# A depthwise convolution's last 128 channels: nine scaled copies on ScalarE summed on GpSimd, in place of block-diagonal matmuls on TensorE

## The chip, the core and the metric

The kernel runs on one core of a Trainium2 chip. The metric is the device time of one execution in microseconds. Before the change three runs gave 7132.22, 7134.73 and 7137.01 us: the median is 7134.73.

The engines are written as in the profile: PE is TensorE (PEld its weight loads), DVE is VectorE, ACT is ScalarE, POOL is GpSimd, SP is SyncE, which here only issues DMAs.

## The reference

The input x is fp32, 16 images of 56 x 56 pixels with 384 channels. Two residual layers follow each other, each behind a group normalisation over 32 groups of 12 channels (mean and variance over a whole image, no learned scale).

```
x = x + proj(dilated_attention(gn(x)))       # layer 0
x = x + conv3x3_depthwise(gn(x), sign(w))    # layer 1
```

- Layer 0: q, k and v are products with a 1152 x 384 matrix. The 384 channels form three sets of 128 with dilation 1, 2 and 3; each set has four heads of 32 channels. Each pixel attends to its nine neighbours at that dilation (zero padding): nine scores, a softmax over them, and the weighted sum of the nine v. Then a 384 x 384 projection and a bias.
- Layer 1: each channel is convolved with its own 3 x 3 kernel, whose nine weights are the signs of w clipped to -1 to 1. So a tap multiplies by 1, -1 or 0. Padding is one pixel of zeros around the normalised image.

## The kernel before

**Tiling.** An image is cut into 7 chunks of 8 rows (PX = 448 pixels), 112 chunks in all. Channels lie on the 128 partitions, in three groups j = 0, 1, 2 of 128 channels; pixels lie along the free dimension.

**Stages.** The loop at the end of the kernel (L487 to L499) calls seven stages for different chunks in one step n: stage_a for n+9 (load, transpose on PE, statistics of layer 0, write to DRAM scratch xd), stage_kv for n+2 (normalise on ACT, k and v products pkv on PE, ACT copies them into the padded tiles kv), stage_s for n+1 (q products pq; DVE products t of q and shifted k; PE sums t over each head with sel into one bank ps), stage_p for n-1 (projection po, residual and bias on DVE into xb, statistics of layer 1, write to the scratch x1d), stage_m for n+1 (softmax), stage_w for n (weighted sum of v), and stage_c for n-9 (the convolution). Layer 1 of an image can only begin when all of layer 0 of that image is done, since its normalisation needs the image's statistics: hence the distance of 9 chunks.

**stage_m.** ACT copies the scores from ps to sT (L349), PE transposes them (pt_s, L358), DVE subtracts the maximum, ACT takes the exponential (L366), DVE divides by the sum. The weights e are split into three bf16 terms: ACT casts (L374, L376), GpSimd subtracts (rest, L375, and the last term of e, L377). PE transposes the terms (pa, L382), ACT copies them (aT, L388).

**stage_w.** For each of the three sets and each of the nine taps, 27 times a chunk: PE spreads the tap's weight over its head's 32 channels (pb_a, L402, two PSUM banks), DVE multiplies by the shifted v (w, L405, five buffers), and GpSimd adds to the set's sum (y, L409: the first add of a set takes two taps, so 8 adds a set and 24 a chunk).

**stage_c.** One DMA brings the chunk's x1 (L446, one buffer). For each j three DMAs (L461) bring the rows shifted by -1, 0 and +1 for 32 channels at a time, so that tile z has 96 partitions, which are 3 row shifts x 32 channels, and four quarters q of 448 pixels; z_p has three buffers. ACT normalises each quarter (L463, mrz holds mean and scale in that layout); GpSimd clears the rows outside the image in the first and the last chunk of an image, before and after (L456, L467). PE then takes 12 matmuls per j (pc, L474): for each column shift kx and quarter q a 96 x 32 matrix kdiag, which has the three row taps on three stacked diagonals, so one matmul sums three taps. The profile counts each fp32 matmul as two records: 72 a chunk. DVE adds pc to x1 (L478). When all three j are there, PE transposes x1 back (pt_o, L482), ACT copies (osb, L484) and a DMA writes the output.

**What orders the work.** The framework's scheduler fixes, when the kernel is built, the order of instructions on each engine's queue, by its own estimate of when they become ready; it also puts in the waits. On the chip each queue runs in that order, and an instruction that waits holds those behind it. DMAs are all issued from SP's queue. Buffers of a pool come round in turn.

Of the kernel before, what the change touches and what calls it, by code (L numbers as in the profile page):

```python
# [8 lines left out]
F32 = mybir.dt.float32  # L9
BF16 = mybir.dt.bfloat16  # L10
AF = mybir.ActivationFunctionType
ALU = mybir.AluOpType
# [4 lines left out]
P = 128  # L17
HEADS = 4
HD = 32
NG = 3  # L20
NTAP = 9
NQ = 4
ROWS = 8
# [9 lines left out]
def dilated_attention_then_binary_conv(  # L33
# [20 lines left out]

    nc = tc.nc
    B, H, W, C = x.shape
    PX = ROWS * W
    NCH = H // ROWS  # L60
# [2 lines left out]
    SCALE = float(HD) ** -0.5  # L63
    DIL = (1, 2, 3)
    K3 = 3 * HD

    xf = x.rearrange("b h w c -> b (h w) c")
    of = out.rearrange("b h w c -> b (h w) c")

    const = ctx.enter_context(tc.tile_pool(name="const", bufs=1))  # L70
# [48 lines left out]
    bias = const.tile([P, NG], F32, name="bias")  # L119

    spread = const.tile([NR, NTAP, P], BF16, name="spread")

    kdiag = const.tile([K3, 3, NG * NQ, HD], F32, name="kdiag")
    with tc.tile_pool(name="setup", bufs=1) as setup:
        wq_in = setup.tile([P, 9, C], F32, name="wq_in")
        nc.sync.dma_start(wq_in, w_qkv.rearrange("(t p) c -> p t c", p=P))
        wp_in = setup.tile([P, 3, C], F32, name="wp_in")
        nc.scalar.dma_start(wp_in, w_proj.rearrange("(t p) c -> p t c", p=P))
        b_in = setup.tile([NG, P], F32, name="b_in")
        nc.scalar.dma_start(b_in, b_proj.rearrange("(j p) -> j p", p=P))  # L130
        k_in = setup.tile([K3, 3, NG * NQ], F32, name="k_in")
        for ky in range(3):
            for kx in range(3):
                nc.scalar.dma_start(
                    k_in[ky * HD : (ky + 1) * HD, kx, :],
                    w_conv[ky, kx].rearrange("(s c) m -> c (s m)", c=HD),
                )

        for cc in range(NG):
            for t3 in range(3):  # L140
                pt = ps_tr.tile([P, 512], F32, tag="tr", name="pt_wq")
                for i in range(3):
# [24 lines left out]

        kc = setup.tile([K3, 3, NG * NQ], F32, name="kc")
        nc.vector.tensor_scalar(kc, k_in, -1.0, 1.0, op0=ALU.max, op1=ALU.min)
        kp = setup.tile([K3, 3, NG * NQ], F32, name="kp")  # L170
        nc.vector.tensor_single_scalar(kp, kc, 0.0, op=ALU.is_gt)
        kn = setup.tile([K3, 3, NG * NQ], F32, name="kn")
        nc.vector.tensor_single_scalar(kn, kc, 0.0, op=ALU.is_lt)
        nc.vector.tensor_sub(kp, kp, kn)
        nc.vector.tensor_sub(kp, kp, kc)
        nc.vector.tensor_add(kp, kc, kp)
        eye3 = setup.tile([K3, HD], F32, name="eye3")
        nc.gpsimd.memset(eye3, 0.0)
        for ky in range(3):
            nc.gpsimd.affine_select(  # L180
                out=eye3, in_=eye3, compare_op=ALU.not_equal, fill=1.0, base=-ky * HD,
                pattern=[[-1, HD]], channel_multiplier=1,
            )
        for kx in range(3):
            nc.vector.tensor_tensor(
                kdiag[:, kx],
                kp[:, kx].unsqueeze(2).to_broadcast([K3, NG * NQ, HD]),
                eye3.unsqueeze(1).to_broadcast([K3, NG * NQ, HD]),
                ALU.mult,
            )  # L190

# [8 lines left out]
    y_p = ctx.enter_context(tc.tile_pool(name="y_p", bufs=5))  # L200
    s_p = ctx.enter_context(tc.tile_pool(name="s_p", bufs=1))
    a_p = ctx.enter_context(tc.tile_pool(name="a_p", bufs=4))
    z_p = ctx.enter_context(tc.tile_pool(name="z_p", bufs=3))
    x1_p = ctx.enter_context(tc.tile_pool(name="x1_p", bufs=1))
    o_p = ctx.enter_context(tc.tile_pool(name="o_p", bufs=2))
    st_p = ctx.enter_context(tc.tile_pool(name="st_p", bufs=2))

# [2 lines left out]
    for g, d in enumerate(DIL):  # L210
        kv.append([])
        for s in range(KV_SLOTS):
            t = const.tile([P, 2, ROWS + 2 * d, W + 2 * d], F32, name=f"kv_{g}_{s}")
            nc.gpsimd.memset(t[:, :, :, 0:d], 0.0)
            nc.gpsimd.memset(t[:, :, :, W + d : W + 2 * d], 0.0)
            kv[g].append(t)

    def rows(ap):
        return ap.rearrange("p (r w) -> p r w", w=W)

    stats0, stats1 = {}, {}
    xd, x1d = {}, {}
    mr0, mr1 = {}, {}
# [38 lines left out]
    def spread_stats(pair):  # L262
        pp = ps_tr.tile([P, 512], F32, tag="tr", name="pp")
        for j in range(NG):
            nc.tensor.matmul(pp[:, 2 * j : 2 * j + 2], gselT[:, j], pair[:, 0:2], start=True, stop=True)
        mr = st_p.tile([P, NG, 2], F32, tag="mr", name="mr", bufs=4)
        nc.vector.tensor_copy(mr.rearrange("p j s -> p (j s)"), pp[:, : 2 * NG])
        return mr
# [144 lines left out]
    def stage_p(n):  # L413

        b, c = divmod(n, NCH)
        if c == 0:
            stats1[b] = st_p.tile([P, NG, NCH, 6], F32, tag="stats1", name="stats1")
            x1d[b] = dr_p.tile([C, H * W], F32, tag="x1d", name="x1d")
        xb, y = xbs.pop(n), ys.pop(n)
        for j in range(NG):  # L420
            po = ps_mm.tile([P, 512], F32, tag="mm", name="po")
            for g in range(NG):
                nc.tensor.matmul(  # L423
                    po[:, :PX], wprojT[:, g, j * P : (j + 1) * P], y[g], start=(g == 0), stop=(g == NG - 1)
                )
            nc.vector.scalar_tensor_tensor(  # L426
                xb[:, j, :], po[:, :PX], bias[:, j : j + 1], xb[:, j, :], op0=ALU.add, op1=ALU.add
            )
            nc.vector.bn_stats(stats1[b][:, j, c, :], xb[:, j, :])
        nc.sync.dma_start(x1d[b].rearrange("(j p) n -> p j n", p=P)[:, :, c * PX : (c + 1) * PX], xb)  # L430
        if c == NCH - 1:
            pair = group_stats(stats1.pop(b))

            mr = spread_stats(pair)
            mrz = st_p.tile([K3, NG, NQ, 2], F32, tag="mrz", name="mrz")
            for ky in range(3):
                for q in range(NQ):
                    nc.sync.dma_start(mrz[ky * HD : (ky + 1) * HD, :, q, :], mr[q * HD : (q + 1) * HD, :, :])
            mr1[b] = mrz

    def stage_c(n):

        b, c = divmod(n, NCH)
        p0 = c * PX
        x1 = x1_p.tile([P, NG, PX], F32, tag="x1", name="x1")
        nc.sync.dma_start(x1, x1d[b].rearrange("(j p) n -> p j n", p=P)[:, :, p0 : p0 + PX])  # L446
        by_set = x1d[b].rearrange("(j q c) n -> j c q n", q=NQ, c=HD)
        for j in range(NG):
            z = z_p.tile([K3, NQ, PX], F32, tag="z", name="z")
            edges = []  # L450
            if c == 0:
# [5 lines left out]
            for ky in range(3):  # L457
                lo = W if c == 0 and ky == 0 else 0
                hi = PX - W if c == NCH - 1 and ky == 2 else PX
                q0 = p0 + (ky - 1) * W  # L460
                nc.sync.dma_start(z[ky * HD : (ky + 1) * HD, :, lo:hi], by_set[j][:, :, q0 + lo : q0 + hi])  # L461
            for q in range(NQ):
                nc.scalar.activation(  # L463
                    z[:, q], z[:, q], AF.Identity, bias=mr1[b][:, j, q, 0:1], scale=mr1[b][:, j, q, 1:2]
                )
            for edge in edges:
                nc.gpsimd.memset(edge, 0.0)  # L467
# [2 lines left out]
            for kx in (1, 0, 2):  # L470
                lo, hi = max(0, 1 - kx), W - max(0, kx - 1)
# [56 lines left out]
```

## Time and profile before

| | |
|---|---|
| median of three runs | 7134.73 us |
| the profiled execution | 7133.72 us, its span 7132.0 us |
| PE busy | 6613.3 us (93%) |
| DVE busy | 4458.9 us (63%) |
| POOL busy | 3364.4 us (47%) |
| ACT busy | 2324.5 us (33%) |
| convolution matmuls (L474) | 8064 records, 1093.8 us busy |
| normalisation for them (L463) | 1344 activations, 753 ns each |
| adds of the weighted sums (L409) | 2688, 1145 and 1136 ns each |
| convolution loads (z from x1d) | 912 DMAs of 224.0 KB, 4.4 us to landing |
| granted PE clock, mean | 0.954 |

The table is of one profiled execution; its span is 1.7 us shorter than its time, and the time is 1 us under the median of the runs. A group of the profile names the line, the engine and operation, output and inputs by the program's names, shapes and count; behind the first bar stand the busy time and the mean duration of one in ns, behind the second the time that the engine sat idle just before them, and what ended most of it. The busy time of matmuls counts overlapping ones once: the four quarters of a pc group run side by side, so 8064 records of 576 ns make only 1093.8 us. The chain is the work that ended last, followed back from the end, at each step to what released it.

### The profile page before, as it was taken

The numbers are of one execution on the slowest core, as the hardware profiler recorded it, in microseconds if no ns is written. First come the engines' busy times: TensorE is split into PE (matmuls) and PEld (weight loads), VectorE is DVE, ScalarE is ACT, GpSimd is POOL, SyncE is SP. The second block draws the span as 40 slices with busy tenths as digits, with TensorE's granted clock in tenths as the row PEclk, the third lists the DMA queues.
The fourth block names the chain that finished last, engine by engine and source line by source line (L and its number), as shares of the span: only waits on it lengthen the run. The fifth ranks groups of instructions, "written<-read, shape, count | busy, mean of one in ns | idle before, by whom it ended". The sixth has DMA issues, their size and how long they took to land.

```text
span 7132.0 us, 88786 instructions
## 1 busy us (share of the span) xinstructions
PE 6613.3 (93%) x30933; PEld 2670.5 (37%) x30933; DVE 4458.9 (63%) x6431; ACT 2324.5 (33%) x4025; POOL 3364.4 (47%) x3279
## 2 busy tenths in 40 slices
PE   6888999999999999999999999999999999999977
PEld 3333333333333333333333333333333333333322
DVE  3666666666666666666666666666666666666650
ACT  2112333333333333333333333333333333333324
POOL 1555444445554544444444555545444444445540
PEclk8889999999999999999999999999999999999977
DMA  3212344333443443344443444343334343333335
GB/s 119 75 55 67 109 117 116 114 108 112 117 114 109 116 113 107 110 113 116 113 114 108 113 113 117 114 115 110 108 110 115 111 116 113 109 98 94 94 96 136
DMA packets 617462, 770.82 MB, mean 108 GB/s; under 512 B 164915, under 2 KB 617014, under 8 KB 617014
## 3 DMA queue, kind: packets, MB, share of 16 engines
q1 hardware_dynamic: 613008, 764.54, 37.8%
q8 instruction: 245, 4.01, 0.2%
q14 instruction: 203, 1.66, 0.1%
q10 hardware_dynamic: 4006, 0.61, 0.1%
HBM read 462.04 MB, written 231.21 MB: 97 GB/s over the span
## 4 chain that ended last, share of the span: by engine, by line
PE 68%; POOL 18%; issue 7%; DVE 5%; DMA 2%; ACT 1%; SPq 0%; POOLq 0%; ACTq 0%; DVEq 0%
PE pkv L310 16%; POOL y L409 15%; PE ps L343 13%; PE po L423 12%; PE pq L330 12%; PE pc L474 6%; PE pb_a L402 4%; DVE w L405 3%; PE pa L382 2%; POOL e L377 1%; PE pt_o L482 1%; PE pt_s L358 1%; PE pt_x L282 1%; DMA z<-x1d 1%; DMA xin<-in_x_dram 1%
## 5 line engine op out<-in xcount | busy, mean ns | idle before, releaser
L409 POOL TENSOR_TENSOR y<-y,w 128x448 f32<-128x448 f32 x2352 | 2693.6, 1145 | 227.4 <-DVE w L405 71.8
L405 DVE TENSOR_TENSOR w<-pb_a,kv 128x448 f32<-128x448 f32 x3024 | 1800.2, 616 | 824.4 <-PE pb_a L402 620.7
L339 DVE TENSOR_TENSOR t<-pq,kv 128x1344 f32<-128x1344 f32 x1008 | 1557.9, 1555 | 951.0 <-PE pq L330 722.0
L310 PE MATMUL pkv<-xn,wqkvT 128*128 128x448 f32 x4032 | 1767.1, 556 | 0.0
L409 POOL TENSOR_TENSOR y<-w 128x448 f32<-128x448 f32 x336 | 381.7, 1136 | 2749.2 <-DVE w L405 2748.7
L474 PE MATMUL pc<-z,kdiag 96*32 96x440 f32 (+1 forms) x8064 | 1093.8, 576 | 38.6 <-ACT z L463 20.0
L402 PE MATMUL pb_a<-aT,spread 108*128 108x448 bf16 x3024 | 1002.4, 371 | 126.3 <-DVE w L405 121.7
L463 ACT ACTIVATE z<-z,mrz 96x448 f32<-96x448 f32 x1344 | 936.0, 753 | 425.0 <-DMA z<-x1d 422.1
L343 PE MATMUL ps<-t,sel 128*32 128x448 f32 x6048 | 963.5, 551 | 0.0
L423 PE MATMUL po<-y,wprojT 128*128 128x448 f32 x2016 | 941.6, 576 | 10.0 <-POOL y L409 10.0
L310 PEld LDWEIGHTS pkv<-xn,wqkvT 128*128 128x128 f32 x4032 | 743.0, 196 | 478.1 <-issue 448.2
L330 PE MATMUL pq<-xn,wqkvT 128*128 128x448 f32 x2016 | 870.4, 557 | 0.0
L313 ACT COPY kv<-pkv 128x448 f32<-128x448 f32 x672 | 360.1, 536 | 910.0 <-PE pkv L310 900.6
L402 PEld LDWEIGHTS <-spread 108*128 108x128 bf16 x3024 | 283.1, 101 | 894.1 <-issue 869.7
L423 PEld LDWEIGHTS po<-y,wprojT 128*128 128x128 f32 x2016 | 329.7, 189 | 623.4 <-issue 608.2
L330 PEld LDWEIGHTS pq<-xn,wqkvT 128*128 128x128 f32 x2016 | 353.5, 189 | 482.6 <-issue 472.5
L349 ACT COPY sT<-ps 128x448 f32<-128x448 f32 x112 | 59.6, 532 | 1434.8 <-PE ps L343 1434.8
L426 DVE SCALAR_TENSOR_TENSOR xb<-po,bias,xb 128x448 f32<-128x448 f32 x336 | 227.0, 676 | 303.4 <-PE po L423 303.3
L343 PEld LDWEIGHTS ps<-t,sel 128*32 128x32 f32 x6048 | 152.3, 108 | 657.4 <-issue 299.6
L474 PEld LDWEIGHTS pc<-z,kdiag 96*32 96x32 f32 x8064 | 224.2, 112 | 459.1 <-issue 354.1
L382 PE MATMUL pa<-ident_h,e 112*108 112x112 bf16 x1344 | 141.6, 259 | 246.9 <-POOL e L377 246.8
L478 DVE TENSOR_TENSOR x<-pc,x 128x448 f32<-128x448 f32 x336 | 207.3, 617 | 228.8 <-PE pc L474 221.2
(90 smaller groups left out, 3556.9 us busy)
## 6 DMA issues: line engine op xcount, KB each, us to landing
z<-x1d SPq DMA_DIRECT2D x912, 224.0 KB, 4.4
xin<-in_x_dram SPq DMA_DIRECT2D x112, 672.0 KB, 6.1
xd<-xa SPq DMA_DIRECT2D x112, 672.0 KB, 5.9
xb<-xd SPq DMA_DIRECT2D x112, 672.0 KB, 4.6
x1d<-xb SPq DMA_DIRECT2D x112, 672.0 KB, 3.1
x<-x1d SPq DMA_DIRECT2D x112, 672.0 KB, 5.4
out_dram<-osb SPq DMA_DIRECT2D x448, 168.0 KB, 2.1
kv<-kv SPq DMA_DIRECT2D x192, 186.0 KB, 2.3
```

What stands on the lines that cost most here:

```text
L310: nc.tensor.matmul(pq[:, :PX], wqkvT[:, cc, o0 : o0 + P], xn[:, cc, :], start=(cc == 0), stop=(cc == NG - 1))
L313: nc.scalar.copy(cur[:, which - 1, d : d + ROWS, d : d + W], rows(pq[:, :PX]))
L330: nc.tensor.matmul(pq[:, :PX], wqkvT[:, cc, g * P : (g + 1) * P], xn[:, cc, :], start=(cc == 0), stop=(cc == NG - 1))
L339: nc.vector.tensor_tensor(t.rearrange("p k (r w) -> p k r w", w=W), q3, k3, ALU.mult)
L343: nc.tensor.matmul(ps[32 * j : 32 * j + 32, :PX], sel[:, s0 : s0 + 32], t[:, kx, :], start=(i == 0), stop=(p + 4 >= NG * NTAP),)
L382: nc.tensor.transpose(pa[:NR, s * SUB : (s + 1) * SUB], e3[:, s * NG + g].rearrange("p t m -> p (t m)"), ident_h[:SUB, :SUB],)
L402: nc.tensor.matmul(pb[:, :PX], spread[:, o, :], aT, start=True, stop=True)
L405: nc.vector.tensor_tensor(rows(w), rows(pb[:, :PX]), vw, ALU.mult)
L409: nc.gpsimd.tensor_tensor(y, first if o == 1 else y, w, ALU.add)
L423: nc.tensor.matmul(po[:, :PX], wprojT[:, g, j * P : (j + 1) * P], y[g], start=(g == 0), stop=(g == NG - 1))
L463: nc.scalar.activation(z[:, q], z[:, q], AF.Identity, bias=mr1[b][:, j, q, 0:1], scale=mr1[b][:, j, q, 1:2])
L474: nc.tensor.matmul(pcr[q * HD : (q + 1) * HD, :, lo:hi], kdiag[:, kx, j * NQ + q, :], zr[:, :, lo + kx - 1 : hi + kx - 1], start=(kx == 1) ...
```

## The change

The convolution of j = 0 and 1 (JG = 2) stays as it was. For j = 2 there is another way:

- At set-up the signs of the nine taps of the last 128 channels are computed into ktap (128 channels x 9). kdiag shrinks to the first two groups. Two padded tiles zg (128 x 10 x 58) are allocated and cleared.
- In stage_c the load of x1 covers j = 0 and 1; a second DMA brings xg, the ten rows of the last 128 channels that the chunk needs (one buffer). ACT normalises xg into the inside of the padded tile zp with one activation. Then ACT makes nine scaled copies of shifted windows of zp, three for each row tap ky, into tiles m (128 x 3 x 448, two buffers). GpSimd adds the second and the third m to the first (1344 elements each), adds the three thirds of the first (two adds of 448), and adds the rows of xg as the residual into x1[:, 2]. That tap code stands ahead of the loop over j.
- z_p goes from three buffers to two.

The same sums are formed, in fp32, in another order. The diff, without the set-up of ktap, which repeats on nine columns the max, min, compare and subtract lines that make kp:

```diff
-    kdiag = const.tile([K3, 3, NG * NQ, HD], F32, name="kdiag")
+    kdiag = const.tile([K3, 3, JG * NQ, HD], F32, name="kdiag")
+
+    ktap = const.tile([P, NTAP], F32, name="ktap")
...
+        nc.sync.dma_start(
+            kg_in, w_conv.rearrange("y x c m -> c (y x m)")[JG * P : (JG + 1) * P, :]
+        )
...
-    z_p = ctx.enter_context(tc.tile_pool(name="z_p", bufs=3))
+    z_p = ctx.enter_context(tc.tile_pool(name="z_p", bufs=2))
     x1_p = ctx.enter_context(tc.tile_pool(name="x1_p", bufs=1))
+    xg_p = ctx.enter_context(tc.tile_pool(name="xg_p", bufs=1))
+    m_p = ctx.enter_context(tc.tile_pool(name="m_p", bufs=2))
...
+    zg = []
+    for s in range(2):
+        t = const.tile([P, ROWS + 2, W + 2], F32, name=f"zg_{s}")
+        nc.gpsimd.memset(t, 0.0)
+        zg.append(t)
...
         x1 = x1_p.tile([P, NG, PX], F32, tag="x1", name="x1")
-        nc.sync.dma_start(x1, x1d[b].rearrange("(j p) n -> p j n", p=P)[:, :, p0 : p0 + PX])
+        nc.sync.dma_start(x1[:, :JG], x1d[b].rearrange("(j p) n -> p j n", p=P)[:, :JG, p0 : p0 + PX])
+        mrz, mr = mr1[b]
         by_set = x1d[b].rearrange("(j q c) n -> j c q n", q=NQ, c=HD)
-        for j in range(NG):
+        lo, hi = (0 if c else 1), ROWS + (2 if c < NCH - 1 else 1)
+        xg = xg_p.tile([P, ROWS + 2, W], F32, tag="xg", name="xg")
+        nc.sync.dma_start(
+            xg[:, lo:hi, :].rearrange("p r w -> p (r w)"),
+            x1d[b][JG * P : (JG + 1) * P, p0 + (lo - 1) * W : p0 + (hi - 1) * W],
+        )
+        zp = zg[n % 2]
+        if c == 0:
+            nc.gpsimd.memset(zp[:, 0], 0.0)
+        if c == NCH - 1:
+            nc.gpsimd.memset(zp[:, ROWS + 1], 0.0)
+        nc.scalar.activation(
+            zp[:, lo:hi, 1 : W + 1], xg[:, lo:hi, :], AF.Identity, bias=mr[:, JG, 0:1], scale=mr[:, JG, 1:2]
+        )
+        taps = []
+        for ky in range(3):
+            m = m_p.tile([P, 3, PX], F32, tag="m", name="m")
+            for kx in range(3):
+                nc.scalar.activation(
+                    rows(m[:, kx]), zp[:, ky : ky + ROWS, kx : kx + W], AF.Copy,
+                    scale=ktap[:, 3 * ky + kx : 3 * ky + kx + 1],
+                )
+            taps.append(m)
+            if ky:
+                nc.gpsimd.tensor_tensor(taps[0], taps[0], m, ALU.add)
+        m = taps[0]
+        for kx in (1, 2):
+            nc.gpsimd.tensor_tensor(m[:, 0], m[:, 0], m[:, kx], ALU.add)
+        nc.gpsimd.tensor_tensor(rows(x1[:, JG]), rows(m[:, 0]), xg[:, 1 : ROWS + 1, :], ALU.add)
+        for j in range(JG):
             z = z_p.tile([K3, NQ, PX], F32, tag="z", name="z")
```

More of the change, by code (lines that the diff above doesn't have):

```diff
@@ L65, in dilated_attention_then_binary_conv @@
     K3 = 3 * HD
+    JG = NG - 1
     xf = x.rearrange("b h w c -> b (h w) c")
@@ L183, in dilated_attention_then_binary_conv @@
             )
+        kg_in = setup.tile([P, NTAP], F32, name="kg_in")
+        nc.sync.dma_start(
+            kg_in, w_conv.rearrange("y x c m -> c (y x m)")[JG * P : (JG + 1) * P, :]
+        )
+        nc.vector.tensor_scalar(kg_in, kg_in, -1.0, 1.0, op0=ALU.max, op1=ALU.min)
+        nc.vector.tensor_single_scalar(ktap, kg_in, 0.0, op=ALU.is_gt)
+        kg_n = setup.tile([P, NTAP], F32, name="kg_n")
+        nc.vector.tensor_single_scalar(kg_n, kg_in, 0.0, op=ALU.is_lt)
+        nc.vector.tensor_sub(ktap, ktap, kg_n)
+        nc.vector.tensor_sub(ktap, ktap, kg_in)
+        nc.vector.tensor_add(ktap, kg_in, ktap)
         for kx in range(3):
@@ L186, in dilated_attention_then_binary_conv @@
                 kdiag[:, kx],
-                kp[:, kx].unsqueeze(2).to_broadcast([K3, NG * NQ, HD]),
-                eye3.unsqueeze(1).to_broadcast([K3, NG * NQ, HD]),
+                kp[:, kx, : JG * NQ].unsqueeze(2).to_broadcast([K3, JG * NQ, HD]),
+                eye3.unsqueeze(1).to_broadcast([K3, JG * NQ, HD]),
                 ALU.mult,
@@ L438, in stage_p @@
                     nc.sync.dma_start(mrz[ky * HD : (ky + 1) * HD, :, q, :], mr[q * HD : (q + 1) * HD, :, :])
-            mr1[b] = mrz
+            mr1[b] = mrz, mr
     def stage_c(n):
@@ L463, in stage_c @@
                 nc.scalar.activation(
-                    z[:, q], z[:, q], AF.Identity, bias=mr1[b][:, j, q, 0:1], scale=mr1[b][:, j, q, 1:2]
+                    z[:, q], z[:, q], AF.Identity, bias=mrz[:, j, q, 0:1], scale=mrz[:, j, q, 1:2]
                 )
```

## The prediction, on record before the result

> **What bounds the kernel now.** I read the page's busy times and groups, then its chain, then where TensorE waits, then one chunk's timeline.
>
> ```profile
> PE 6613.3 (93%) x30933; PEld 2670.5 (37%) x30933; DVE 4458.9 (63%) x6431; ACT 2324.5 (33%) x4025; POOL 3364.4 (47%) x3279
> PE 68%; POOL 18%; issue 7%; DVE 5%; DMA 2%; ACT 1%; SPq 0%; POOLq 0%; ACTq 0%; DVEq 0%
> L409 POOL TENSOR_TENSOR y<-y,w 128x448 f32<-128x448 f32 x2352 | 2693.6, 1145 | 227.4 <-DVE w L405 71.8
> L474 PE MATMUL pc<-z,kdiag 96*32 96x440 f32 (+1 forms) x8064 | 1093.8, 576 | 38.6 <-ACT z L463 20.0
> L463 ACT ACTIVATE z<-z,mrz 96x448 f32<-96x448 f32 x1344 | 936.0, 753 | 425.0 <-DMA z<-x1d 422.1
> ```
>
> By busy time TensorE is the bound, but 18% of the chain is GpSimd. Three windows of one chunk, then the waits of TensorE from 1000 to 6800 us, show why:
>
> ```profile
> 4262.00:4285.00 23.00, 23.00 (x93) 7.38 (x91) 16.16 (x13) 5.39 (x9) 0.00 (x0) 1.00 0.02 4
> 4285.00:4297.00 12.00, 10.51 (x84) 2.89 (x82) 9.84 (x18) 1.67 (x3) 7.91 (x8) 1.00 0.58 177
> 4297.00:4311.00 14.00, 13.29 (x68) 7.24 (x69) 9.05 (x16) 9.28 (x18) 12.66 (x12) 0.88 0.26 76
> ```
>
> ```profile
> PE pa L382 <- POOL e L377: 201.4, 96, 4.5
> PE pb_a L402 <- DVE w L405: 81.4, 188, 1.0
> ```
>
> (Columns: length, then busy time and count of PE, weight loads, DVE, ACT, POOL; clock; DMA.) A chunk has two parts. In one of about 31 us (kv and q products, scores, projection) TensorE is full and GpSimd idle. In the other, the **tap stretch**, 27 broadcasts pb_a go TensorE, DVE (w), GpSimd (24 adds y, through 5 w buffers), and the convolution's pc matmuls fill TensorE's gaps. TensorE waits there on GpSimd: at pa for the softmax's last piece e, at pb_a for w buffers. GpSimd's own timeline there:
>
> ```profile
> 4288.51 1.14 POOL L409 TENSOR_TENSOR y<-w 128x448 f32<-128x448 f32 x1 [27.67 <-DVE w L405]
> 4289.73 1.15 POOL L409 TENSOR_TENSOR y<-y,w 128x448 f32<-128x448 f32 x1
> 4291.31 1.37 POOL L409 TENSOR_TENSOR y<-y,w 128x448 f32<-128x448 f32 x1 [0.42 <-DVE w L405]
> 4292.64 1.01 POOL L375 TENSOR_TENSOR rest<-e,e 112x432 f32<-112x432 f32 x1
> 4293.61 2.35 POOL L409 TENSOR_TENSOR y<-y,w 128x448 f32<-128x448 f32 x2
> 4295.92 1.00 POOL L377 TENSOR_TENSOR e<-rest,e 112x432 bf16<-112x432 f32 x1
> 4296.89 3.54 POOL L409 TENSOR_TENSOR y<-y,w 128x448 f32<-128x448 f32 x3
> 4301.07 1.13 POOL L409 TENSOR_TENSOR y<-w 128x448 f32<-128x448 f32 x1 [0.64 <-DVE w L405]
> ```
>
> It is nearly gapless from its first add, and pa starts when e ends:
>
> ```profile
> 4294.55 0.94 PE L474 MATMUL pc<-z,kdiag 96*32 96x440 f32 x8
> 4296.98 0.80 PE L382 MATMUL pa<-ident_h,e 112*108 112x112 bf16 x8 [1.49 <-POOL e L377]
> ```
>
> So the stretch is paced by GpSimd, and the matmuls to be removed lie in it.
>
> [...] the add beside DVE's e<-e,sm took 1.37 us instead of 1.14. [...] after the wait at pa the granted clock was 0.50 from 4298 to 4300 us.
>
> **The change, part by part** (per chunk; 112 chunks, 103 of which have a tap stretch beside a convolution).
>
> TensorE loses a third of L474: 1093.8/3/112 = 3.26 us. At face value 365 us in all. But the order of the built kernel keeps the broadcasts, kv products and transposes where they were: only pc is gone, ahead of pa. pa comes when GpSimd's e ends, and e's inputs (pt_s, DVE, ACT casts) are unchanged. So there the 1.5 us wait becomes about 4 to 5, and the 3.26 us are worth nothing. DVE loses one 0.62 us add, which was not late.
>
> GpSimd gains two adds of 1344 [...], two folds and a last add into x1 (1.145 each): 9.5 us, 1060 in all. In the built order the first four lie behind the chunk's last y and ahead of the next first y (108 of 112), in the hole of 27.67 us. Only the last add lies inside the y sequence, behind 14 or 16 of 24 adds in 87 chunks: **+1.15 us on the pacing engine**. It waits for the transposes pt_o of the chunk before, placed behind broadcast 20; by the w buffers that broadcast can go out once add 13 is done, some 1.9 us ahead, so I charge nothing. If late, everything behind it (y, w, pb_a) stalls as long.
>
> What is given back: over 74 regular chunks (not first or last of an image) I took the marks of the 65 such stretches of the middle. GpSimd idles 2.1 us inside the y sequence, of which about 1.0 is issue gaps and 0.4 the first w. The rest, near 0.7, comes from late broadcasts behind pa; eleven broadcasts now lie ahead of pa instead of ten, and no pc behind it. The add that frees w buffers for the last two broadcasts ends 26.9 us after pt_s; gapless it would be 26.6, plus 1.15 = 27.75, so +0.8. The last broadcast follows it by 2.15 us, where 0.62 (w) + 0.3 (pb_a) + 0.75 (one kv product) = 1.65 suffice: -0.5. **Net +0.3 us x 74 = +22.** Bounds: -0.45 (both gaps vanish) and +1.15 (none): -33 to +85. In 29 chunks at image ends the last add is behind the y sequence, and a z memset goes: 0, bounds -15 to +30.
>
> ScalarE loses four activations of 753 and gains one of 560 elements [...] and nine of 448 [...]: +3.7 us per chunk, 415 in all, to 38%. They stand behind the kv copies and ahead of sT, the copy that starts the softmax. The order has ScalarE wait before the seventh tap for GpSimd's first 1344 add (two m buffers); sT and all behind it would be held. Time: kv copies end near 4262.2, four z to 4265, one to 4266, six taps to 4269.5, the add to 4272.5, three taps to 4274.5, second add and folds to 4280. sT is at 4283.3, the next first add at 4346. Slack 9 us: nothing. If xg comes late this cover is gone, microsecond for microsecond.
>
> DMA and SP: three z loads (4.4 us to landing) go and one of xg comes; x1 shrinks by a third. xg is queued on SP behind xin and ahead of the x1d write and the next z loads, which a late xg would hold; it waits for the last add of the chunk before, over by then: xin is issued after the last pt_x, some 5 us behind that add. z_p drops to two buffers for two tiles: same reuse distance. Nothing.
>
> **The end** has no cover. There the last chunks run convolution alone, 22.2 us each from 7010.6 to 7099.3. Now one xg buffer closes a ring: last add, then SP issues xg and behind it three z loads (0.4 + 1.3), landing 5.7, four z activations 2.7, one 0.85, six taps 3.7, add 3.0, three taps 1.8, add 3.0, folds 2.3, last add 1.15 = 25.9, with semaphores 26.5. **+4.3 x 8 = +34**, bounds +5 and +60. Set-up (a small load, six DVE operations, two memsets) lies beside the first 145 us: 0 to 3.
>
> Sum against the profiled execution (7133.7, span 7132.0, 1 below the median 7134.7): 7133.7 + 22 + 0 + 34 = **7190**.
>
> **The rivals.** (a) TensorE's lost work is lost time: 7134 - 365 = 6770. For it: 93% busy, 68% of the chain. Against: pa's wait. A smaller form, deciding the other side: if the y gaps all go (-33) and the end hides its ring (+5), and image ends gain 15, 7090; it decides from 1.15 us of recovered GpSimd idle time per chunk. (b) The last add is paid in full, none recovered[...]: 103 x 1.2 + 34 = 158, 7290. (c) ScalarE's in-order wait holds sT in each chunk by 5 us: 103 x 5 + 34, 7680. Against: 9 us slack. (d) The change does less than it says: not possible, the order shows the work moved.
>
> **How the numbers follow.** Forecast (7150 to 7235) 0.5; its neighbour within 0.2% of 7134 (about what a measurement can tell from no change) 0.12; (a) 0.12, nearly all in its small form; (b) up to 7300, 0.2; (c) 0.06. The range 7105 to 7290 leaves out (c), the top of (b) and the deep part of (a). Faster 0.12, same 0.12, slower 0.76.
>
> **What would show it.** PE busy down by some 350 us with the span not; TensorE's wait for e at pa up from 2.1 to 4 or 5 us a chunk; the two 1344 adds near 3.0 us each and in the hole; sT still waiting for ps, not queued behind taps; about 26 us per chunk at the end. I am wrong if pa's wait stays small (then TensorE was pacing), if sT follows directly on a tap, or if GpSimd waits at the last add for pt_o.

## The result, and the profile after

The changed kernel takes 7155.8 us (median of four runs, 7155.48 to 7160.27) beside 7134.45 us of the kernel before on the same chip: ratio 1.0031, 95% interval 1.0014 to 1.0049. It is slower, by 21 us; 56 were forecast. The profiled execution has a span of 7154.4 us, 22.4 more than before.

First the page: the engines' busy times, the chain's shares and the groups that the change touches.

```profile
PE 6404.7 (90%) x28245; PEld 2695.7 (38%) x28245; DVE 4392.0 (61%) x6325; ACT 2700.7 (38%) x4697; POOL 4402.6 (62%) x3809
PE 69%; POOL 16%; issue 6%; DVE 6%; DMA 2%; ACT 1%; SPq 0%; POOLq 0%; DVEq 0%; ACTq 0%
L497 POOL TENSOR_TENSOR m<-m 128x1344 f32<-128x1344 f32 x224 | 681.8, 3044 | 1134.5 <-ACT m L491 1134.5
L528 PE MATMUL pc<-z,kdiag 96*32 96x440 f32 (+1 forms) x5376 | 715.5, 558 | 51.4 <-POOL z L521 31.1
L491 ACT ACTIVATE m<-zg,ktap 128x448 f32<-128x448 f32 x1008 | 589.9, 658 | 371.8 <-POOL m L497 367.6
```

The work moved as announced: TensorE is busy 209 us less, GpSimd 1038 us more, ScalarE 376 us more. (The pc group itself lost 378 us; TensorE's other instructions took 170 us more, at a mean granted clock of 0.936 instead of 0.954.) The 1344 add takes 3044 ns, a tap 658 ns. (The forecast's 3.0 us for the add was shown by no trace of before, and so it is with its sums of 9.5 us a chunk on GpSimd and 3.7 on ScalarE; 1038 and 376 us are 9.3 and 3.4 a chunk.) GpSimd has 31% more busy time and the chain holds less of it. So where did 22 us come from? The waits of TensorE between 1000 and 6800 us:

```profile
PE pa L406 <- POOL e L401: 285.0, 95, 4.9
PE pb_a L426 <- DVE w L429: 156.7, 295, 1.5
```

Both grew, from 201.4 and 81.4: TensorE now waits 159 us more on the engines that pace it. The same three windows of a chunk as before (length; busy time and count of PE, weight loads, DVE, ACT, POOL; clock; DMA share; GB/s):

```profile
4246.00:4269.00 23.00, 23.00 (x93) 7.38 (x92) 16.17 (x13) 10.67 (x17) 8.35 (x4) 1.00 0.18 51
4269.00:4281.00 12.00, 9.70 (x67) 2.65 (x65) 11.23 (x20) 2.46 (x5) 8.18 (x9) 1.00 0.57 173
4281.00:4295.00 14.00, 11.90 (x56) 7.42 (x57) 6.97 (x13) 7.90 (x16) 12.71 (x13) 0.76 0.26 67
```

In the first, TensorE is as full as before (23.00 of 23.00) while GpSimd, idle there before, now does four adds in 8.35 us. In the two windows of the tap stretch TensorE is busy 2.2 us less; that the stretch does not shorten is measured further down. GpSimd's timeline in that chunk shows the new adds in their places:

```profile
4257.02 3.04 POOL L497 TENSOR_TENSOR m<-m 128x1344 f32<-128x1344 f32 x1 [15.28 <-ACT m L491]
4262.03 3.04 POOL L497 TENSOR_TENSOR m<-m 128x1344 f32<-128x1344 f32 x1 [1.97 <-ACT m L491]
4265.15 2.35 POOL L500 TENSOR_TENSOR m<-m 128x448 f32<-128x448 f32 x2
4272.51 1.15 POOL L433 TENSOR_TENSOR y<-w 128x448 f32<-128x448 f32 x1 [5.02 <-DVE w L429]
...
4289.86 4.79 POOL L433 TENSOR_TENSOR y<-y,w 128x448 f32<-128x448 f32 x4 [0.78 <-DVE w L429]
4294.61 1.14 POOL L501 TENSOR_TENSOR x<-m,xg 128x448 f32<-128x448 f32 x1
4295.71 1.13 POOL L433 TENSOR_TENSOR y<-w 128x448 f32<-128x448 f32 x1
```

Four of the five end 5.02 us before the first y; the fifth (L501) stands between two sums of y. TensorE's lines up to pa in that chunk:

```profile
4278.40 0.35 PE L426 MATMUL pb_a<-aT,spread 108*128 108x448 bf16 x1 [0.75 <-DVE w L429]
4278.94 0.35 PE L426 MATMUL pb_a<-aT,spread 108*128 108x448 bf16 x1 [0.18 <-DVE w L429]
4279.54 0.35 PE L426 MATMUL pb_a<-aT,spread 108*128 108x448 bf16 x1 [0.25 <-DVE w L429]
4283.10 0.99 PE L406 MATMUL pa<-ident_h,e 112*108 112x112 bf16 x8 [3.21 <-POOL e L401]
```

pa still starts when GpSimd's e ends, after a wait of 3.21 us instead of 1.49. That is where part of TensorE's removed time lies.

To see where the 22 us are I cut each profiled execution at two marks that every kernel here has: the first pt_s (the softmax's first transposes) of the first chunk and of the 112th. What lies ahead is the start, what lies between them the middle, what follows the end. The end holds the last tap stretch and nine chunks that have convolution alone. Times are read off the trace, in us:

```
                          start   middle    end     sum
before                    145.1   6685.6   301.3   7132.0
after                     151.7   6739.6   263.0   7154.4
difference                 +6.6    +54.0   -38.3    +22.4
```

So the small result is a loss of 60 us and a gain of 38 us. Inside the middle, a chunk's period can be cut once more at its last broadcast pb_a: the stretch ahead of it, paced by GpSimd, and the tail behind it, where TensorE is full. Over 65 chunks of the middle that are not at an image's end (13 images of five), and for the two periods per image that are (kv matmuls counted as the profile's records, 36 a chunk):

```
                          stretch   tail   kv matmuls in the tail   image-end pair
before                     29.08    31.15         18.77                125.33
after                      29.24    31.56         19.94                126.26
```

The stretch grew by 0.16 us, the tail by 0.41 (more kv matmuls stand in it), together 0.57 x 74 = 42; the image ends give 0.93 x 15 = 14. That is the 54 us within 2.

The traces say more of both parts. In the tail TensorE stands idle for less than 0.1 us and its granted clock is 1.00, before and after; all that it does more after is 1.17 kv records (eight take 3.17 us in a fence further down, so some 0.46 us), and 0.4 of a small statistics product has left it. In the stretch TensorE's idle time grew by 2.0 us a chunk (2.77 to 4.82), and its mean granted clock fell from 0.958 to 0.905: 41 of the 65 stretches hold two spells of 3.4 us at half clock, where before 6 did. After, in the chunk of the fences above, two pkv records took 1.70 us at a granted clock of 0.50 (from 4284.63 us) and 0.92 at 1.00 (from 4289.34). By these clocks TensorE stands at half clock for 3.1 us more (estimated: 2 x 0.095 x 29.24 less 2 x 0.042 x 29.08) and does some 1.6 us less work there. So the 3.26 us taken from it became idle time and a slower clock, not a shorter stretch; most of the 170 us that its other instructions took more can be explained in this way.

At the end, before, ScalarE waited for z loads; after, it waits less for them, and besides for xg and for GpSimd. The first fence is ScalarE before; the second and third are ScalarE and GpSimd after; each in one chunk that has no other work beside it:

```profile
7021.20 2.71 ACT L463 ACTIVATE z<-z,mrz 96x448 f32<-96x448 f32 x4 [5.62 <-DMA z<-x1d]
7024.29 2.72 ACT L463 ACTIVATE z<-z,mrz 96x448 f32<-96x448 f32 x4 [0.38 <-DMA z<-x1d]
```

```profile
7077.79 2.71 ACT L517 ACTIVATE z<-z,mrz 96x448 f32<-96x448 f32 x4 [2.64 <-DMA z<-x1d]
7081.56 0.85 ACT L484 ACTIVATE zg<-xg,mr 128x560 f32<-128x560 f32 x1 [1.05 <-DMA xg<-x1d]
7082.51 3.46 ACT L491 ACTIVATE m<-zg,ktap 128x448 f32<-128x448 f32 x6
```

```profile
7077.46 1.13 POOL L501 TENSOR_TENSOR x<-m,xg 128x448 f32<-128x448 f32 x1
7086.05 3.02 POOL L497 TENSOR_TENSOR m<-m 128x1344 f32<-128x1344 f32 x1 [7.46 <-ACT m L491]
7091.03 3.03 POOL L497 TENSOR_TENSOR m<-m 128x1344 f32<-128x1344 f32 x1 [1.96 <-ACT m L491]
7094.14 2.33 POOL L500 TENSOR_TENSOR m<-m 128x448 f32<-128x448 f32 x2
7096.55 1.14 POOL L501 TENSOR_TENSOR x<-m,xg 128x448 f32<-128x448 f32 x1
```

From one last add to the next are 7096.55 - 7077.46 = 19.1 us. The forecast had 26.5 for this ring, and 22.2 before. The loads took, from issue to landing (the first line is before, 7010 to 7100 us; the others after, 7060 to 7130):

```profile
z<-x1d SPq DMA_DIRECT2D x35, 224.0 KB, 5.7
z<-x1d SPq DMA_DIRECT2D x22, 224.0 KB, 4.3
xg<-x1d SPq DMA_DIRECT2D x2, 280.0 KB, 3.0
```

### The profile page after: what moved, and what is told of

Same layout as the page of the kernel before. It is cut to its first block, busy times and chain, and to the rows that moved or that the text cites. A ratio compares the mean times of both kernels' runs of the same rounds, so it can differ in the third digit from the quotient of the medians.

```text
span 7154.4 us, 83789 instructions
## 1 busy us (share of the span) xinstructions
PE 6404.7 (90%) x28245; PEld 2695.7 (38%) x28245; DVE 4392.0 (61%) x6325; ACT 2700.7 (38%) x4697; POOL 4402.6 (62%) x3809
## 4 chain that ended last, share of the span: by engine, by line
PE 69%; POOL 16%; issue 6%; DVE 6%; DMA 2%; ACT 1%; SPq 0%; POOLq 0%; DVEq 0%; ACTq 0%
PE pkv L334 17%; POOL y L433 12%; PE ps L367 12%; PE po L447 12%; PE pq L354 11%; PE pb_a L426 5%; PE pc L528 5%; DVE w L429 3%; PE pt_o L536 2%; PE pa L406 2%; POOL e L401 1%; PE pt_s L382 1%; PE pt_x L306 1%; DMA z<-x1d 1%; POOL m L497 1%
## 5 line engine op out<-in xcount | busy, mean ns | idle before, releaser
L334 PE MATMUL pkv<-xn,wqkvT 128*128 128x448 f32 x4032 | 1829.4, 572 | 0.0
L497 POOL TENSOR_TENSOR m<-m 128x1344 f32<-128x1344 f32 x224 | 681.8, 3044 | 1134.5 <-ACT m L491 1134.5
L426 PE MATMUL pb_a<-aT,spread 108*128 108x448 bf16 x3024 | 1029.1, 385 | 228.8 <-DVE w L429 205.2
L334 PEld LDWEIGHTS pkv<-xn,wqkvT 128*128 128x128 f32 x4032 | 765.1, 203 | 521.4 <-issue 500.8
L528 PE MATMUL pc<-z,kdiag 96*32 96x440 f32 (+1 forms) x5376 | 715.5, 558 | 51.4 <-POOL z L521 31.1
L491 ACT ACTIVATE m<-zg,ktap 128x448 f32<-128x448 f32 x1008 | 589.9, 658 | 371.8 <-POOL m L497 367.6
L517 ACT ACTIVATE z<-z,mrz 96x448 f32<-96x448 f32 x896 | 638.7, 756 | 69.5 <-DMA z<-x1d 65.3
L406 PE MATMUL pa<-ident_h,e 112*108 112x112 bf16 x1344 | 156.0, 278 | 341.2 <-POOL e L401 340.0
L373 ACT COPY sT<-ps 128x448 f32<-128x448 f32 x112 | 59.6, 532 | 802.0 <-PE ps L367 802.0
```

Of the source, the lines that this page charges most:

```text
L334: nc.tensor.matmul(pq[:, :PX], wqkvT[:, cc, o0 : o0 + P], xn[:, cc, :], start=(cc == 0), stop=(cc == NG - 1))
L426: nc.tensor.matmul(pb[:, :PX], spread[:, o, :], aT, start=True, stop=True)
L491: nc.scalar.activation(rows(m[:, kx]), zp[:, ky : ky + ROWS, kx : kx + W], AF.Copy, scale=ktap[:, 3 * ky + kx : 3 * ky + kx + 1],)
L497: nc.gpsimd.tensor_tensor(taps[0], taps[0], m, ALU.add)
L517: nc.scalar.activation(z[:, q], z[:, q], AF.Identity, bias=mrz[:, j, q, 0:1], scale=mrz[:, j, q, 1:2])
L528: nc.tensor.matmul(pcr[q * HD : (q + 1) * HD, :, lo:hi], kdiag[:, kx, j * NQ + q, :], zr[:, :, lo + kx - 1 : hi + kx - 1], start=(kx == 1) ...
```

## The experiments

My theory after the result: TensorE's removed time is worth next to nothing in the middle; the middle pays for the last add in the y sequence and for kv matmuls that the build moved into the tail; the end gains because nothing hides the convolution there. Rivals: the middle pays for the lower PE clock (0.97 before, 0.95 after between 1000 and 6800 us), for the lost z buffer, or for the adds in the hole; the end gains by something the middle hands over. Thirteen kernels were run; the medians of before were 7133.07, 7134.91, 7135.47 and 7134.05 us in the four groups of runs. Each ratio is to the before of the same group, with its 95% interval; start, middle and end are of the profiled execution.

**The last add on VectorE** (e1).

```diff
-        nc.gpsimd.tensor_tensor(rows(x1[:, JG]), rows(m[:, 0]), xg[:, 1 : ROWS + 1, :], ALU.add)
+        nc.vector.tensor_tensor(rows(x1[:, JG]), rows(m[:, 0]), xg[:, 1 : ROWS + 1, :], ALU.add)
```

> The last add of the tap path (m + xg into x1) is put on VectorE; the four others stay on GpSimd. Theory (the add lies in GpSimd's y sequence and is paid there, partly out of idle time; the rest of the middle's +54 us is kv products that moved into the tail): the y sequence gives back what it grew by, 0.16 us a chunk by the broadcasts and up to 0.66 by the last-but-two add, so 12 to 50 us off the steady part, 7105 to 7145 us. Rival (the steady part grew because TensorE runs at 0.95 instead of 0.98 of its clock): no GpSimd instruction matters, 7150 to 7160 us. Rival (the add blocks VectorE's queue of products while it waits for the folds): slower than 7160 us.

Measured: 7139.1 us (ratio 1.0007, 0.9999 to 1.0015), start 150.0, middle 6718.6, end 268.5. The stretch fell from 29.24 to 28.62 us, the tail stayed (31.55). So the add costs 0.62 us a chunk more on GpSimd than on VectorE, and the clock rival falls: the clock is no higher here (0.94) and the regular chunks are back at before's time. But the image-end pair rose to 128.73. There the add stands in VectorE's queue:

```profile
3615.15 0.62 DVE L429 TENSOR_TENSOR w<-pb_a,kv 128x448 f32<-128x448 f32 x1 [5.17 <-PE pb_a L426]
3621.05 0.63 DVE L501 TENSOR_TENSOR x<-m,xg 128x448 f32<-128x448 f32 x1 [5.28 <-PE pt_o L536]
```

It waited 5.28 us for the transposes pt_o to release the one x1 buffer.

**The add split between the two engines** (e11) tested that wait.

```diff
-        nc.gpsimd.tensor_tensor(rows(x1[:, JG]), rows(m[:, 0]), xg[:, 1 : ROWS + 1, :], ALU.add)
+        (nc.gpsimd if c >= NCH - 2 else nc.vector).tensor_tensor(rows(x1[:, JG]), rows(m[:, 0]), xg[:, 1 : ROWS + 1, :], ALU.add)
```

> The changed kernel with the last add on VectorE in the first five chunks of an image and on GpSimd in the last two (there the add on VectorE stood 5.3 us in front of products, waiting for x1's buffer). Theory: regular chunks as with the add on VectorE (-0.05 us against before), the two image-end chunks as in the changed kernel (+0.9 us per image), so steady part +5 to +20, end -35, start +5: 7105 to 7125 us. Rival (image-end chunks suffer from the order of the build, not from that wait): as with the add on VectorE throughout, 7135 to 7142 us.

Measured: 7136.2 us (1.0001, 0.9992 to 1.0009), start 150.7, middle 6711.9, end 274.2. A miss, and on the rival's side: the image-end pair came down only from 128.73 to 127.80 instead of to 126.3, and the end was nearly 6 us longer. So the wait explains some four tenths of what the add on VectorE cost there; the rest I put down to the order that the build gives these chunks, which I have not taken further apart.

**The removal alone** (e5): the kernel before, with the third group's convolution left out and nothing in its place.

```diff
-        for j in range(NG):
+        for j in range(NG - 1):
             z = z_p.tile([K3, NQ, PX], F32, tag="z", name="z")
```

> The kernel before with the convolution of the third group left out and nothing in its place (its channels pass through x1 unchanged): the removal alone. Theory (TensorE's removed time lies beside GpSimd's sums and is worth nothing in the steady part; the end has no such cover and gets shorter): regular chunks -0.3 to +0.3 us, start 0, end -40 to -60, so 7070 to 7105 us. Rival (TensorE's 365 us were on the path): 6770 us; in its small form (half of it) 6950 us.

Measured: 7062.89 us (0.9898, 0.9884 to 0.9911), start 146.7, middle 6663.7, end 244.5. That is 7 us under the range of the theory. Of the 77 us that its profiled execution is shorter than before's, 22 are in the middle and 57 in the end. In a regular chunk the stretch fell by 0.86 us, and the tail rose by 0.41, to the 31.56 us and 19.94 kv matmuls of the changed kernel. So the kv matmuls move because the third group's work is gone (its pc has left the gaps, as I read it), not because of the taps. The clock rival falls here too: the stretch has the low clock of the changed kernel (0.90) and is shorter. The changed kernel's stretch is 1.02 us longer than this one: 0.62 of that the last add on GpSimd, the rest not divided further. The image-end pair is 126.74, above before's 125.33, with less work; I put that down to the build's order too. TensorE's wait at pa between 1000 and 6800 us, of this kernel:

```profile
PE pa L382 <- POOL e L377: 288.0, 96, 3.7
```

As after (285.0). The removed 365 us of TensorE went for the most part into waits at pa and in the stretch and into its slower clock; the rival that had them on the path (6770 us, or 6950) is out.

**No adds in the hole** (e6): the changed kernel without L497 and L500.

```diff
-            if ky:
-                nc.gpsimd.tensor_tensor(taps[0], taps[0], m, ALU.add)
...
-        for kx in (1, 2):
-            nc.gpsimd.tensor_tensor(m[:, 0], m[:, 0], m[:, kx], ALU.add)
```

> The changed kernel without the two 1344 adds and the two folds on GpSimd (only the last add stays, so eight of nine tap products are left out of the sum). Theory (the four adds lie in GpSimd's hole and cost the steady part nothing; in the end they are 8.4 us of a ring of 19.1 us per chunk): steady part as in the changed kernel within 10 us, end 20 to 60 us shorter, 7095 to 7140 us. Rival (the hole adds are what the steady part pays for, at image ends above all): steady part 40 to 55 us shorter as well, 7040 to 7090 us.

Measured: 7142.73 us (1.0012, 1.0006 to 1.0019), start 149.4, middle 6749.0, end 247.5. The middle gained nothing (+9), stretch and tail are 29.26 and 31.56 as in the changed kernel; the end is 15.5 us shorter, less than the 20 to 60 expected, and so the time lies 3 us above the range. The four adds, 8.4 us a chunk and some 940 us of busy GpSimd, cost the middle nothing. In the end they are 8.4 of the 19.1 us of the ring, and yet without them the last chunks still come 17.2 us apart (17.0 in the kernel of the removal alone, which has no xg): another limit stands just behind the ring.

**The lost z buffer** (e3): the kernel before with two.

```diff
-    z_p = ctx.enter_context(tc.tile_pool(name="z_p", bufs=3))
+    z_p = ctx.enter_context(tc.tile_pool(name="z_p", bufs=2))
```

> The kernel before with z_p of 2 buffers instead of 3, nothing else. Theory (the buffer is not part of the cost): 7128 to 7150 us, the end at most some us longer. Rival (the lost buffer is what costs the steady part 54 us): 7170 us or more.

Measured: 8507.27 us (1.1923, 1.1907 to 1.194). By its number that is the rival's side, but a loss of 1374 us is not the rival's 54. With three groups a chunk and two buffers, the third group's matmuls come late, and the build puts the kv matmuls behind them: of 36 a chunk only 2.8 stay in the stretch (17.23 before) and 33.2 stand in the tail, and with them all transposes pt_x and 7.4 of 12 pt_o. The tail grows from 31.15 to 39.66 us (the stretch from 29.08 to 34.80). TensorE's timeline in one such chunk from the last broadcast on, without the lines of the transposes (one chunk in five has 14 pc records behind the last broadcast, as here; the others have none):

```profile
4301.18 0.56 PE L402 MATMUL pb_a<-aT,spread 108*128 108x448 bf16 x1
4301.66 3.16 PE L474 MATMUL pc<-z,kdiag 96*32 96x440 f32 x14
4304.75 2.81 PE L310 MATMUL pkv<-xn,wqkvT 128*128 128x448 f32 x4
...
4307.61 0.92 PE L310 MATMUL pkv<-xn,wqkvT 128*128 128x448 f32 x2
...
4309.02 3.17 PE L310 MATMUL pkv<-xn,wqkvT 128*128 128x448 f32 x8
```

All behind the last pb_a, where nothing is free. In the changed kernel two tiles use the two buffers and this doesn't happen: the removal alone (e5), with three buffers, has the same tail. So the buffer is not what its middle pays for; but the run shows in large what 1.2 moved kv matmuls do in small.

**The tap path in the last 9 chunks only** (e2, and e4 with three z buffers), and **everywhere but there** (e2b).

```diff
+        JC = JG if n >= N - 9 else NG
...
-        for j in range(JG):
+        for j in range(JC):
```

> Tap path for the last 9 chunks only, the ones that have no other work beside them; TensorE convolves all three groups in the other 103 chunks (z_p of 2, one padded buffer instead of two). Theory (the end is where the change gains, and the steady part is where it loses): start +6, steady part 0, end about -40, so 7095 to 7110 us. Rival (the end got shorter only because the work arrives in another order from the steady part, the first interval of 30.9 us among it): end about -22 or less, 7115 to 7140 us. Rival (z_p of 2 is what the steady part pays for): 7150 us or more.

Measured: 8480.26 us (1.1885, 1.1869 to 1.1901), for the reason just shown: on its own it decides nothing, but it is 27 us shorter than the 8507.27 of e3.

> Tap path for the last 9 chunks alone again, now with the three z buffers that the kernel before has; the tap products take t's buffers, which are idle by then. Theory (the gain of the change lies in the end, its loss in the start and the steady part): start +3 to +6, steady part 0, end about -40, so 7095 to 7110 us. Rival (the end is shorter only because of what the steady part hands over to it): 7120 us or more.

Measured: 7112.41 us (0.9969, 0.9958 to 0.9981), start 148.6, middle 6683.2, end 277.3. The middle is before's, the end gains 24 us instead of 40, so the time is 2 us above the theory's range, and this kernel is faster than both.

> The converse: tap path for the first 103 chunks, all three groups on TensorE in the last 9. Theory: start +6, steady part +54, end 0 (z_p of 2 may make it a little worse), so 7185 to 7205 us. Rival (the end does not depend on the path of its own chunks): 7150 to 7165 us.

Measured: 7193.44 us (1.0081, 1.0067 to 1.0095), start 148.4, middle 6745.9, end 299.3. All of the loss, none of the gain. The two halves together: middle -2.4 and +60.3, end -24.0 and -2.0. The end's remaining 12 us appear only when both have the tap path.

**One chunk more** (e13) asked for those 12 us.

```diff
-        JC = JG if n >= N - 9 else NG
+        JC = JG if n >= N - 10 else NG
```

> Tap path in the last 10 chunks instead of the last 9: the one more is the last chunk that has other work beside it; the products take xa's buffers, idle by then. Theory (14 of the 38 us that the end gained are handed over by that chunk: one z group less to be normalised and loaded in front of the 12 mrz transfers): end -34 to -40 against before, start +4, 7095 to 7106 us. Rival (they come from elsewhere in the steady part): as with 9 chunks, 7110 to 7116 us.

Measured: 7110.26 us (0.9966, 0.9954 to 0.9979), start 149.5, middle 6688.7, end 273.3. A miss, and the rival's time: end -28, not -34 to -40, and the middle 5 us longer than with 9 chunks. (The tap products lie in other buffers than in e4.) So one chunk hands over 4 us of it and pays for them. Where the other 8 us come from stays open.

**What paces the end** (e9 with taps, e10 without). Both give the last 9 chunks two x1 buffers and send the last image's mrz transfers from ScalarE's queue; e9 also has two xg and two padded buffers and the last add on VectorE.

```diff
-        x1 = x1_p.tile([P, NG, PX], F32, tag="x1", name="x1")
+        x1 = (xa_p if n >= N - 9 else x1_p).tile([P, NG, PX], F32, tag="xa" if n >= N - 9 else "x1", name="x1")
...
-                    nc.sync.dma_start(mrz[ky * HD : (ky + 1) * HD, :, q, :], mr[q * HD : (q + 1) * HD, :, :])
+                    (nc.scalar if b == B - 1 else nc.sync).dma_start(mrz[ky * HD : (ky + 1) * HD, :, q, :], mr[q * HD : (q + 1) * HD, :, :])
```

> Tap path in the last 9 chunks alone, with what the traces show to hold it up there taken away: x1 in two buffers (xa's, idle by then), two xg and two padded buffers, the last image's 12 mrz transfers on ScalarE's queue instead of SP's, the last add on VectorE; the load of the tap weights goes to ScalarE's queue. Theory (the end is a set of rings over single buffers and SP's queue): start +1 to +4, steady part 0, end 15 to 40 us shorter than in the run with the tap path in the last 9 chunks, so 7070 to 7100 us. Rival (the end is paced by ScalarE's normalisations and TensorE, not by rings): 7105 to 7115 us.

> The control: the kernel before with the same two buffers for x1 in the last 9 chunks and the last image's mrz transfers on ScalarE's queue, no tap path at all. If the tap path is what shortens the end: 7115 to 7135 us, at least 20 us above its partner with taps. If the rings are all of it: within 10 us of its partner.

Measured: 7112.17 us (0.9969, 0.9957 to 0.998) and 7118.87 us (0.9977, 0.9967 to 0.9986). With taps nothing was won over e4, as the rival had it: all these single buffers opened at once were no help. Without taps the second x1 buffer and the moved transfers were worth 17 us. The two stand 7 us apart; on record, under 10 was to speak for the rings and not for the taps: much of what the taps win at the end can be had without them. So taps or buffers each take the end to 19 or 20 us a chunk, and both together do no better. What is left in e9 is a circle through two in-order queues. ScalarE's osb copy stands behind six taps; SP's store of osb waits for the copy, and behind the store stand the next loads:

```profile
7040.49 3.47 ACT L492 ACTIVATE m<-zg,ktap 128x448 f32<-128x448 f32 x6
7043.86 0.83 ACT L539 COPY osb<-pt_o 112x384 f32<-112x384 f32 x2
```

```profile
7044.35 0.80 SPq L540 DMA_DIRECT2D out_dram<-osb  x2
7045.24 0.39 SPq L516 DMA_DIRECT2D z<-x1d  x1
7049.91 1.34 SPq L540 DMA_DIRECT2D out_dram<-osb  x2
7051.31 0.91 SPq L516 DMA_DIRECT2D z<-x1d  x2
7052.33 0.38 SPq L470 DMA_DIRECT2D x<-x1d  x1
7052.75 0.47 SPq L476 DMA_DIRECT2D xg<-x1d  x1
```

That reading is argued from the order; I have not broken this circle by a run.

**A second xg buffer** (e7; one padded buffer instead of two, to make room), and **the same without the adds in the hole** (e12, whose further edit is that of e6).

```diff
-    xg_p = ctx.enter_context(tc.tile_pool(name="xg_p", bufs=1))
+    xg_p = ctx.enter_context(tc.tile_pool(name="xg_p", bufs=2))
```

> The changed kernel with two xg buffers instead of one (and one padded buffer zp instead of two, to make room). Theory (the end's pace of 19.1 us per chunk is the ring last add, xg load, normalise, taps, adds): steady part unchanged, end chunks at 14 to 17 us, so 7110 to 7140 us. Rival (the end is paced by z loads, ScalarE or TensorE, the ring only looks closed): 7150 to 7160 us.

Measured: 7519.8 us (1.0539, 1.0525 to 1.0554), start 148.3, middle 7107.7, end 265.6. Neither: the middle lost 368 us, and the end as a whole hardly moved. (Its last chunks did come closer, 17.9 us apart instead of 19.1, so the ring with one xg buffer did set that pace; those ahead of them came later.) (The single padded buffer is in e2b too, whose middle is 6745.9; so it is the xg buffer.) GpSimd in one chunk, then ScalarE and TensorE in the same chunk:

```profile
4515.59 4.78 POOL L433 TENSOR_TENSOR y<-y,w 128x448 f32<-128x448 f32 x4
4520.33 3.02 POOL L497 TENSOR_TENSOR m<-m 128x1344 f32<-128x1344 f32 x1
4523.30 2.35 POOL L433 TENSOR_TENSOR y<-y,w 128x448 f32<-128x448 f32 x2
4525.60 3.05 POOL L497 TENSOR_TENSOR m<-m 128x1344 f32<-128x1344 f32 x1
```

```profile
4523.38 1.79 ACT L491 ACTIVATE m<-zg,ktap 128x448 f32<-128x448 f32 x3 [5.25 <-POOL m L497]
4525.07 0.94 ACT L337 COPY kv<-pkv 128x448 f32<-128x448 f32 x2
```

```profile
4525.63 4.78 PE L354 MATMUL pq<-xn,wqkvT 128*128 128x448 f32 x12 [1.31 <-ACT kv L337]
```

With xg there early, the build has the taps ahead of the kv copies. The seventh tap waits 5.25 us for the first 1344 add, which now stands between sums of y; the kv copies wait behind the tap, and TensorE behind a copy. That is the hold-up of ScalarE that the prediction's third rival had at sT, at another instruction. 65 of 182 such adds of the middle lie between sums of y here, none in the changed kernel.

> Two xg buffers, as in the run that lost 368 us in the steady part, but without the two 1344 adds and the two folds on GpSimd (eight of nine tap products are left out of the sum). Theory (the second xg buffer lets the taps come early, so the 1344 adds fall into the y sequence instead of the hole, and that is the loss): steady part back to that of the changed kernel within 25 us, 7120 to 7165 us. Rival (the loss is ScalarE's early taps in front of its other work, or the order of the build, whatever GpSimd does): 7400 us or more.

Measured: 7237.14 us (1.014, 1.0125 to 1.0156), middle 6838.4, end 249.7. Between the two: without the adds 269 of the 368 us come back, so they and the waits for them are nearly three quarters of the loss; 99 us remain, of the taps' early place on ScalarE or of the order (20.71 kv matmuls in the tail instead of 19.94). The run doesn't tell which.

## Why the prediction missed

The side was right and the time inside the range, but a loss of 56 us was forecast and 21 came. The step that failed is **the end**: +34 forecast, -38 measured. It hides a second error in the other direction, in the middle and the start.

1. *TensorE's 365 us are worth nothing in the tap stretch.* Right. Removal alone gave 22 us in the middle. pa waits for e; but the wait grew from 2.1 to 3.0 us a chunk, not to 4 or 5, because TensorE also waits more at pb_a, ahead of pa too (0.18 to 0.75 us a broadcast in the chunk shown), and stands longer at half clock.
2. *Two 1344 adds and two folds in the hole: free.* Right, size (3044 ns) and place; without them the middle gained nothing. The cover is narrower than it looked: where the taps come earlier, the same adds are most of a 368 us loss. The one xg buffer, which looked like a cost, is what holds them in the hole.
3. *The last add, +0.8 by its 1.15 less 0.5 recovered: +0.3 x 74 = +22.* The mechanism holds: the stretch grew by 0.16 us, and the add costs 0.62 more there than on VectorE. The term lacks what the same step denied, that kv products stay where they were. The build moved 1.2 kv matmuls a chunk out of the gaps that pc had left and into the tail: +0.41, more than the stretch. So 42 us came and not 22.
4. *Image ends 0 (-15 to +30).* +14, inside the bounds. The removal alone has it too (+1.4 us a pair), so it is not the taps.
5. *ScalarE and sT: nothing.* Right. ScalarE still waits for the scores ahead of each sT (802.0 us in 112 chunks), so no tap holds it; in the chunk shown the last tap is done 5.43 us ahead, where 9 had been reckoned.
6. *The end: +4.3 x 8 = +34.* The failed step. The ring is there, but two of its terms were wrong. xg lands 3.0 us after issue; I had used 5.7, which the z and x loads took at the old end, where there were more of them. And the four z activations (2.7) and the three z loads (1.3) are not in it: the z group that ScalarE normalises ahead of zp was loaded before xg, so it runs while xg lands. That leaves 19.8; measured are 19.1. Against it stood 22.2 before, which is itself a wait: ScalarE waited for z loads (5.62 us in the fence above, 2.64 after), and the one x1 buffer had a part in it, since e10, with as many loads, comes to 20.3 a chunk. 19.1 less 22.2 over 8 chunks is -25, and the tap path in the last 9 chunks alone gives -24; with the tap path throughout it is -38. Of the difference 4 us come from the chunk before, 2 appear in the converse kernel, and 8 stay open. I bounded this step from +5 up and thought of no way for it to be negative: I compared a new ring with an old pace without asking what made the old pace.
7. *Start 0 to 3.* +6.6 in the changed kernel's profile; the other kernels with the same set-up have +3 to +6, those without it +1 to +3.

Rival (a) in its small form, 7090, had +5 for the end and gains of 48 us in the middle. The end was far shorter than that; the middle, +54, decided against it. Its large form, (b) and (c) are out by their numbers. A second spell of half clock did come in 41 of 65 stretches, but not the price of (b): the removal alone has that spell too, in 42 of 65, and its stretch is shorter.

The halved clock is in the trace, and its length: 0.50 for 3.41 us in the chunk of the prediction and for 6.83 us in that chunk after. The waits at pa there were 1.49 and 3.21 us. What sets the halving off is not shown: no run here varies that wait alone.

## What to carry to other kernels

Before pricing a stage by its new ring, say what sets its old pace; work that is hidden in the steady part may be all that counts in the prologue or the tail, and can be changed there alone (here -0.3%, where everywhere it is +0.3%). Work taken off an engine that waits may free gaps and little time (here the removal of TensorE's 365 us shortened the middle by 22), and a scheduler that fills queues anew may move other work out of those gaps (1.2 kv matmuls a chunk). A buffer is also a brake that decides where work falls: one more made this kernel 5% slower, one less made its predecessor 19% slower.

## What I had not expected of the hardware

- The same load did not always take the same time to land. In the last chunks an xg load of 280 KB landed in 3.0 us and a z load of 224 KB in 4.3 us; before, with nine z loads a chunk instead of six, z took 5.7. Between 2000 and 6000 us the same xg load took 5.1. No run here parts the number of loads from their order and timing.
- At an image's end VectorE was the worse place for a short add although it has slack (e1): in its queue the 0.63 us add waited 5.1 us on average for pt_o (71.2 us in 14 waits) in front of the products, where GpSimd's own wait for it was 2.8 us (42.5 us in 15 waits). In the whole kernel the add still costs less on VectorE (6 us above before, where the changed kernel is 21).
